# A planned four-layer graph kernel: seven more turns of 128x512 tiles by VectorE and DMA in place of TensorE, with new planning constants

## The chip, the cores and the metric

The kernel runs on one core of one Trainium2 chip. The metric is the device time of one execution in microseconds, as the median of several runs. Everything is float32.

## The reference

The input x has 64 graphs of 256 nodes with 128 features, and all graphs share one symmetric 256x256 adjacency matrix. Four layers follow one another, each as x = layernorm(x + layer(x)):

```python
# layer 0: attention whose logits come from pairs of nodes, softmax over axis 1
h = x @ Wo; att = softmax(where(adj > 0, leaky(u1[idx1] + u2[idx2]), NEG), axis=1)
out0 = att @ h + x @ Wself
# layer 1: attention with source and target terms, then elu
att = softmax(where(adj + I == 0, NEG, leaky(es[:, None] + ed[None, :])))
out1 = elu(att @ (x @ W))
# layer 2: five steps of a gated recurrent cell, with m = adj @ h in both halves of av
z = sigmoid(av @ w3.T + h @ u3.T); r = sigmoid(av @ w4.T + h @ u3.T)
h = (1 - z) * h + z * tanh(av @ w5.T + (r * h) @ u5.T)
# layer 3: x W0 + sums of adj^k x Wk, k = 1, 2, 3, once for each of two adjacencies (here the same)
```

## The kernel before

**Units and lanes.** Two graphs make a unit: 512 rows of 128 features, 32 units (NU), which take their buffers from ten lanes (unit u uses lane u % 10). Ten units are open at a time; when one ends, the next of its lane begins, and its x is loaded when its predecessor's tasks have been spawned.

**The planner.** The kernel first writes down every instruction of a unit as a task with an engine, an estimated duration and its dependencies (`Plan.add`, L94). `Plan.run` (L156) then plays the five queues (TensorE, VectorE, ScalarE, GpSimd and SP, which issues the DMAs) forward in estimated time, and on each engine that is free takes the ready task with the smallest key. The order it writes out is the program's order on every engine; the hardware then runs each engine in that order and waits where data isn't there. The key is made by `first` (L1184): the unit's number times PERIOD (for the last ten units a value that differs by only TAIL = 0.3 of a PERIOD from unit to unit), plus the task's due time, minus HASTE for the engines that HASTE names, if the task lies between the first and the last use of a PSUM bank (`within`). The due time is the estimated length of the chain before the task in its unit, times PACE (PACE_GATED in layer 2). Setup tasks that are wanted late have a rank in place of the key. LATENCY is the assumed time from an instruction's end to where its result can be used, 4000 ns for a DMA; in the first 35 us (START) the shorter table EARLY is used. TURN is added to a VectorE task of the kind [...], if the one before it was of that kind too.

**Two layouts.** A state is used with rows on the partitions (as the stationary operand of a product with the adjacency) and with features on the partitions (for the products with weights). So states are turned again and again, in one of two ways:

- By TensorE: four transposes of 128x128 into a PSUM bank and one ScalarE copy out of it (`feature_major`, L590, whose transposes are L593 and whose copy is L595; in layer 2, L1031 and L1034).
- By VectorE and DMA ("far"): a VectorE transpose of 32x32 blocks (L606, L1006 or L1019), a store to a DRAM buffer hb (L609, L1009 or L1024), and loads that bring the blocks to their places (four of 64 KB at L612 or L1012; one at L1027 behind four stores).

`far(u, step)` (L585) says which way a unit takes at a step. Step -1 is the turn into layer 2, steps 0 to 4 are those of layer 2, step 5 is the turn into layer 3. All units are far at all steps, but units 0 and 1 only from step 2 on (FIRST_FAR), and unit 31 only at steps below 1, that is -1 and 0 (LAST_FAR).

**The input.** `load_x` (L360) brings a unit's x into the lane's buffer m. Units below XDIRECT = 10 load it in one DMA with rows on the partitions (L364); layer 0 turns it by TensorE (L713). From unit 10 on, four DMAs (L368) bring it in with its 32-wide blocks placed so that one VectorE transpose (L714) finishes the turn. The loads of units 0 to 9 are in the setup, before other work on SP. Unit 0's goes out on ScalarE's queue. In layer 0, L727 multiplies x with the weights, L798 and L803 make the output; on units from 3 on, small vectors are spread over the partitions through DRAM rows (L620, L624, L743).

**Filler.** `warm` (L401) issues 256-wide matmuls of the identity (L405), four at the start and six that carry a rank behind all else.

**Layer 2.** In each of five steps m = adj @ h is made in one of two ways. Where `far(u, step - 1)` holds, `left_fast` (L899) takes seven 128-wide products (L904) with three block sums on GpSimd (L893, L895, L896) and merges (L936 to L939); else `left` (L877) takes four 256-wide ones (L881) and a ScalarE copy (L959). Five 512-wide products with the gates' weights follow (L963), with three tanh on ScalarE and four VectorE updates.

**Layer 3.** Its products with the weights and with the squared adjacency are made in one of two ways. Units below NU - PLAIN = 28 use `layer3_blocks` (L1064): 21 products of 128 columns (L1088), with seven GpSimd operations (L1080, L1121 to L1123), seven copies (L1099) and VectorE sums (L1102, L1135). Units 28 to 31 use `layer3_end` (L1148): eight 256-wide products with the weights (L1157), two copies (L1161) and four 256-wide products (L1164). The last two units end with `layernorm_last` (L683), in halves.

Of the kernel before, what the change touches and what calls it, by code (L numbers as in the profile page):

```python
# [28 lines left out]
DIRECT_D = 3  # L29
WARM = 6  # L30
FIRST_FAR = {0: 2, 1: 2}
LAST_FAR = {0: 1}
PERIOD = 41000.0
TAIL = 0.3
LATE = 5
PACE = 4.0
PACE_GATED = 1.56
HOLD = 80
DIRECT_ROWS = 3
XDIRECT = 10  # L40
START = 35e3
HASTE = {"pe": 45000.0, "act": 45000.0}
IN_PSUM = (0, 1, 0, 1)
MARGIN = {}
TURN = 12000.0
PLAIN = 4
R2 = 1
R3 = 1.5

# [25 lines left out]
class Plan:  # L75
# [2 lines left out]

    LATENCY = {"pe": 400, "dve": 350, "act": 350, "pool": 900, "sp": 4000}

    EARLY = {"pe": 250, "dve": 180, "act": 200, "pool": 250, "sp": 2500}
    OWN = {"pe": 0, "dve": 70, "act": 70, "pool": 100}
# [71 lines left out]
    def run(self, spawn, units, key):  # L156
# [23 lines left out]
        def start(lane):  # L180
            mine = [u for u in queue if u % LANES == lane]
            if mine:
# [5 lines left out]
                for t in self.tasks[seen:]:  # L188
                    t.due = max([d.due + (PACE_GATED if t.layer == 2 else PACE) * (d.ns + (
                        d.wait + self.LATENCY["sp" if d.dma else d.eng] if d.dma or d.eng != t.eng else self.OWN[t.eng]))  # L190
                        for d in t.deps if d.unit == t.unit], default=0.0)
# [6 lines left out]
        while any(ready.values()) or running:  # L198
# [11 lines left out]
            for e, tasks in ready.items():  # L210
# [4 lines left out]
                if not fit:  # L215
                    continue
                t = min(fit, key=lambda t: key(t) + (TURN if twice and t.port and e == "dve" else 0))
                if t.at > now:
# [10 lines left out]
                if t.port:  # L229
                    held[e] = t.off - 65 if e == "dve" else begin + 50 if t.ns > 900 else t.off - 125  # L230
                t.end = t.off + (self.EARLY if now < START else self.LATENCY)["sp" if t.dma else e] + t.wait
                done_at[t] = t.end
# [18 lines left out]
def kernel(  # L251
# [108 lines left out]
    def load_x(u, by="sp"):  # L360
        z = lanes[u % LANES]["m"]
        if u < XDIRECT:
            queue = {"sp": nc.sync, ACT: nc.scalar}[by]
# [209 lines left out]
    def gd(ap):  # L573
        return ap.rearrange("p (g d) -> p g d", g=G)
# [10 lines left out]
    def far(u, step):  # L585


        return step >= FIRST_FAR.get(u, -1) and step < LAST_FAR.get(NU - 1 - u, STEPS + 1)

    def feature_major(src, view, t):  # L590
        ps = bank()
        for g in range(G):
            add(PE, 110, lambda g=g: nc.tensor.transpose(ps.ap[:, g * P : (g + 1) * P], view(g), ident.ap),  # L593
                (src, ident), (ps,))
        add(ACT, 475, lambda: nc.scalar.copy(t.ap, ps.ap), (ps,), (t,))  # L595
# [113 lines left out]
    def layer0(u, L):  # L709
        xT, z = L["xT0"], L["m"]  # L710
        if u < XDIRECT:
            feature_major(z, lambda g: gd(z.ap)[:, g], xT)
# [333 lines left out]
    def layer3(u, L):  # L1046
# [10 lines left out]

        if u >= NU - PLAIN:
            layer3_end(u, L, xT, aT, s, tail)
# [88 lines left out]
    def layer3_end(u, L, xT, aT, s, tail):  # L1148
        ps = [bank() for _ in range(NC)]

        def view(c):
            return ps[c].ap.rearrange("p (k b d) -> p k b d", k=2, b=UB)

        for k, src in enumerate((xT, aT)):
            for c in range(NC):
                for b in range(UB):
                    add(PE, mm_ns(N), lambda k=k, src=src, c=c, b=b: nc.tensor.matmul(  # L1157
                        view(c)[:, :, b, :], bn(src.ap)[:, b, c * P : (c + 1) * P], w3.ap[:, k],
                        start=(k == 0 and b == 0), stop=(k == 1), skip_group_check=True), (src, w3), (ps[c],), tail)
        for c in range(NC):  # L1160
            add(ACT, 300, lambda c=c: nc.scalar.copy(s.ap[:, c * N : (c + 1) * N], ps[c].ap[:, N : 2 * N]), (ps[c],), (s,), group=ps)  # L1161
        for c in range(NC):
            for mc in range(NC):
                add(PE, mm_ns(N), lambda c=c, mc=mc: nc.tensor.matmul(  # L1164
                    ps[c].ap[:, 0:N], a2T.ap[:, mc, c * P : (c + 1) * P], s.ap[:, mc * N : (mc + 1) * N],
                    start=False, stop=(mc == NC - 1), skip_group_check=True), (a2T, s), (ps[c],))
        pairs = [(ps[c], lambda c=c: view(c)[:, 0]) for c in range(NC)]
        if u >= NU - 2:
            layernorm_last(u, pairs)
            return  # L1170
        layernorm(u, L, pairs, swap=True)
        add("sp", 450, lambda: nc.sync.dma_start(out_u[u], X[u].ap), (X[u],), ())
# [10 lines left out]
    def first(t):  # L1183
        if t.rank is not None:  # L1184
            return t.rank * PERIOD
        if t.unit < 0:
            return t.due - 1e6
        soon = HASTE.get(t.eng, 0) if t.within else 0
        return (t.unit if t.unit < NU - LANES else NU - 1 - LATE - (NU - 1 - t.unit) * TAIL) * PERIOD + t.due - soon
# [34 lines left out]
```

The softmax here doesn't subtract the row's maximum and nothing guards it: scores larger than these inputs give would overflow.

## Time and profile before

| what | value |
|---|---|
| median of 3 runs | 1382.91 us (1382.16 to 1383.07) |
| the profiled execution | 1382.03 us |
| its span, first to last instruction | 1380.2 us, granted TensorE clock 1.00 |
| TensorE busy | 1371.9 us (99%), 7221 instructions |
| VectorE, ScalarE, GpSimd busy | 1167.7 (85%), 972.2 (70%), 691.3 us (50%) |
| DMA | 147.21 MB, 107 GB/s; q1, SP's queue, 46.8% of 16 engines |
| layer 2's weight products (L963), 1600 instructions | 593 ns a record |
| transposes of x in layer 0 (L593 on m), 40 instructions | 273 ns a record |
| VectorE transposes of x (L714), 22 | 0.70 us each |

An f32 matmul appears as two instructions, a transpose as one. Records of TensorE overlap, since matmuls are pipelined, and their ends are modelled: what an instruction costs TensorE is the distance to the start of the next one. A timeline row merges neighbours of the same kind: start, time to the end of the last of them, engine, line, operation, names, shape, count, and in brackets the idle time of the engine before it. In the table of stretches, the columns after the stretch's length are the busy us (and instructions) of TensorE, its weight loads, VectorE, ScalarE and GpSimd, then the granted clock, the DMA share and GB/s. A buffer's number is left out of its name, so units are told apart by time and line only.

### The profile page before, as it was taken

How to read it: one execution, taken by the hardware profiler on the slowest of the kernel's cores; microseconds unless marked ns; L12 is line 12 of the kernel's file. 1: busy time of each engine (PE TensorE's matmuls, PEld its weight loads, DVE VectorE, ACT ScalarE, POOL GpSimd, SP SyncE). 2: the span in 40 equal slices, each digit the busy share in tenths (PEclk: the TensorE clock that was granted, in tenths of full speed). 3: DMA queues.
4: the chain of work that ended last, by engine and by line, in shares of the span. 5: the costliest groups of instructions: out<-in, count | busy, mean ns of one | idle time of the engine just before them, and what ended most of it. 6: DMA issues, size and time to landing. Idle time of an engine off the chain costs nothing.

```text
span 1380.2 us, 24466 instructions
## 1 busy us (share of the span) xinstructions
PE 1371.9 (99%) x7221; PEld 970.5 (70%) x7221; DVE 1167.7 (85%) x2709; ACT 972.2 (70%) x2414; POOL 691.3 (50%) x1240
## 2 busy tenths in 40 slices
PE   9999999999999999999999999999999999999998
PEld 9767676676676776767767667776666676667777
DVE  7968988988888888899888998888888787889854
ACT  6897676756776777778777767788766656566555
POOL 5214473544554664556545564565545433446814
PEclk9999999999999999999999999999999999999999
DMA  4223454454455455454555455545555443645412
GB/s 128 56 55 89 105 117 114 98 126 106 107 131 108 92 117 137 109 118 105 109 126 119 112 111 110 109 107 134 119 114 117 90 103 84 131 111 117 109 47 69
DMA packets 530084, 147.21 MB, mean 107 GB/s; under 512 B 456480, under 2 KB 495136, under 8 KB 529952
## 3 DMA queue, kind: packets, MB, share of 16 engines
q1 hardware_dynamic: 529152, 145.13, 46.8%
q8 instruction: 58, 0.95, 0.3%
q14 instruction: 74, 0.61, 0.2%
q10 hardware_dynamic: 800, 0.52, 0.1%
HBM read 81.10 MB, written 64.46 MB: 105 GB/s over the span
## 4 chain that ended last, share of the span: by engine, by line
PE 98%; DVE 1%; ACT 0%; issue 0%; POOL 0%; POOLq 0%; DVEq 0%; ACTq 0%
PE ps L963 50%; PE ps L904 20%; PE ps L1088 10%; PE ps L840 4%; PE ps L803 4%; PE ps L727 2%; PE ps L852 2%; PE ps L798 2%; PE ps L881 1%; PE ps L1157 1%; PE ps L1164 0%; PE ps L405 0%; PE ps L593 0%; PE ps L1031 0%; PE ps L636 0%; PE ps L752 0%
## 5 line engine op out<-in xcount | busy, mean ns | idle before, releaser
L963 PE MATMUL ps<-m,gT 128*128 128x512 f32 x960 | 473.3, 593 | 0.0
L963 PEld LDWEIGHTS ps<-m,gT 128*128 128x128 f32 x960 | 168.0, 191 | 131.8 <-issue 114.4
L975 ACT ACTIVATE e<-ps,bias 128x512 f32<-128x512 f32 x160 | 109.8, 687 | 94.7 <-PE ps L963 85.8
L649 POOL TENSOR_SCALAR ve<-st 128x4 f32<-128x4 f32 x110 | 26.8, 244 | 278.4 <-DVE st L647 269.6
L963 PE MATMUL ps<-e,u5T 128*128 128x512 f32 x320 | 163.5, 592 | 0.0
L904 PEld LDWEIGHTS ps<-adjTp,ht 128*128 128x128 f32 x726 | 118.6, 191 | 61.2 <-issue 48.6
L652 POOL TENSOR_TENSOR rstd<-ve,nhalf 128x4 f32<-128x4 f32 x126 | 137.5, 1091 | 47.5 <-DVE ve L649 41.4
L993 ACT ACTIVATE p<-ps,bias 128x512 f32<-128x512 f32 x160 | 109.9, 687 | 66.6 <-PE ps L963 64.2
L904 PE MATMUL ps<-adjTp,e 128*128 128x128 f32 x968 | 149.0, 276 | 0.2 <-ACT m L919 0.2
L984 ACT ACTIVATE ps<-ps,bias 128x512 f32<-128x512 f32 x160 | 105.6, 661 | 55.1 <-PE ps L963 54.3
L893 POOL TENSOR_TENSOR e<-ht 128x256 f32<-128x256 f32 x121 | 96.9, 801 | 88.1 <-DMA ht<-hb 73.1
L904 PEld LDWEIGHTS ps<-adjTp,e 128*128 128x128 f32 x968 | 129.6, 192 | 11.9 <-issue 7.9
L996 DVE SCALAR_TENSOR_TENSOR ps<-ps,p 128x512 f32<-128x512 f32 x160 | 110.2, 689 | 32.0 <-ACT p L993 31.4
L904 PE MATMUL ps<-adjTp,ht 128*128 128x128 f32 x726 | 136.7, 275 | 0.0
L963 PEld LDWEIGHTS ps<-e,u5T 128*128 128x128 f32 x320 | 58.7, 190 | 63.1 <-issue 55.5
L963 PE MATMUL ps<-xT,gT 128*128 128x512 f32 x192 | 98.2, 593 | 0.0
L671 ACT ACTIVATE x<-ht,ve,rstd 128x128 f32<-128x128 f32 x208 | 91.1, 490 | 5.1 <-POOL ve L660 5.0
L936 DVE TENSOR_TENSOR m<-ps,m 128x256 f32<-128x256 f32 x182 | 74.8, 413 | 14.1 <-PE ps L904 12.8
L829 ACT ACTIVATE e<-m,esd 128x256 f32<-128x256 f32 x116 | 84.6, 769 | 0.0
L978 DVE SCALAR_TENSOR_TENSOR e<-e,xT 128x512 f32<-128x512 f32 x96 | 72.2, 752 | 12.9 <-ACT e L975 12.4
L893 POOL TENSOR_TENSOR e<-x 128x256 f32<-128x256 f32 x61 | 48.6, 797 | 65.5 <-ACT x L671 57.7
L919 ACT COPY m<-ps 128x128 f32<-128x128 f32 x182 | 48.0, 268 | 44.0 <-PE ps L904 35.0
(219 smaller groups left out, 3356.1 us busy)
## 6 DMA issues: line engine op xcount, KB each, us to landing
hb<-p SPq DMA_DIRECT2D x182, 256.0 KB, 2.3
ht<-hb SPq DMA_DIRECT2D x484, 64.0 KB, 2.6
xT<-hb SPq DMA_DIRECT2D x244, 64.0 KB, 2.6
m<-row SPq DMA_DIRECT2D x58, 256.0 KB, 3.7
hb<-p SPq DMA_DIRECT2D x124, 64.0 KB, 1.8
ht<-hb SPq DMA_DIRECT2D x31, 256.0 KB, 2.8
out_dram<-x SPq DMA_DIRECT2D x30, 256.0 KB, 2.4
m<-in_x_dram SPq DMA_DIRECT2D x88, 64.0 KB, 2.4
```

Of the source, the lines that this page charges most:

```text
L652: add(POOL, 1010, lambda: nc.gpsimd.tensor_tensor(rstd.ap, ve.ap, nhalf.ap, op=ALU.pow), (ve, nhalf), (rstd,))
L671: add(ACT, 400, lambda j=j, b=b, ch=ch, view=view, at=at, shift=shift, col=col: nc.scalar.activation(X[u].ap[:, b, ch, :], view()[:, j, :] ...
L829: add(ACT, 660 if u >= DIRECT_ROWS else 360, lambda g=g, b=b: nc.scalar.activation(e.ap[:, g, :].rearrange("p (c n) -> p c n", c=NC), ev() ...
L893: add(by, wide, lambda: eng.tensor_sub(four[:, 0:2], blk(slice(2, 3)).to_broadcast([P, 2, D]), blk(slice(0, 4, 3))), (src,), (s,), group=s ...
L904: add(PE, mm_ns(P) + 4, lambda: nc.tensor.matmul(ps.ap[:, at * P : (at + 1) * P], lhs(), mat.ap[:, k, c * P : (c + 1) * P], start=start, s ...
L936: add(DVE, 335, lambda: nc.vector.tensor_tensor(mv[:, 1:3], pv(y)[:, 0:2], mv[:, 3:4].to_broadcast([P, 2, P]), op=ALU.add), (y, m), (m,))
L963: add(PE, mm_ns(T), lambda: nc.tensor.matmul(ps.ap, w(), rhs.ap, start=start, stop=stop, skip_group_check=True), (c, rhs), (ps,), after)
L975: add(ACT, 590, lambda ps_g=ps_g, up=up, tr=tr: nc.scalar.activation(tr.ap, ps_g.ap, AF.Tanh, bias=bias2.ap[:, 1:2], scale=0.5 / up), (ps_ ...
L984: add(ACT, 590, lambda ps_g=ps_g, up=up, tz=tz: nc.scalar.activation(tz.ap, ps_g.ap, AF.Tanh, bias=bias2.ap[:, 0:1], scale=0.5 / up), (ps_ ...
L993: add(ACT, 590, lambda ps_v=ps_v, up=up, tv=tv: nc.scalar.activation(tv.ap, ps_v.ap, AF.Tanh, bias=bias2.ap[:, 2:3], scale=1 / up), (ps_v, ...
L996: add(DVE, 600, lambda tz=tz, tv=tv, vv=vv: nc.vector.scalar_tensor_tensor(vv.ap, tz.ap, 1.0, tv.ap, op0=ALU.add, op1=ALU.mult), (tv, tz), ...
L1088: nc.tensor.matmul(part(ps, at)[:, 0], l(), r(), start=start, stop=True, skip_group_check=True)
```

## The change

Seven constants are changed:

```diff
-LAST_FAR = {0: 1}
+LAST_FAR = {0: 3}
...
-PACE = 4.0
+PACE = 3.0
...
-XDIRECT = 10
+XDIRECT = 5
 START = 35e3
-HASTE = {"pe": 45000.0, "act": 45000.0}
+HASTE = {"pe": 70000.0, "act": 70000.0, "dve": 70000.0}
 IN_PSUM = (0, 1, 0, 1)
 MARGIN = {}
-TURN = 12000.0
-PLAIN = 4
+TURN = 0
+PLAIN = 3
...
-    LATENCY = {"pe": 400, "dve": 350, "act": 350, "pool": 900, "sp": 4000}
+    LATENCY = {"pe": 400, "dve": 350, "act": 350, "pool": 900, "sp": 3500}
```

Three of them change instructions. With XDIRECT = 5 the x of units 5 to 9 comes in by four DMAs and is turned by VectorE (L368 and L714) in place of one DMA, four transposes and a copy. With LAST_FAR = 3 unit 31 is far at steps 1 and 2 too: the states after these steps are turned by VectorE and DMA, and steps 2 and 3 use `left_fast`. With PLAIN = 3 unit 28 uses `layer3_blocks`. The other four (PACE, HASTE, TURN and the DMA entry of LATENCY) enter only the planner's estimates and keys, so the order of the instructions on every engine is another one throughout.

## The prediction

> **What bounds the kernel now.** I read the page first: the busy line and the chain that ended last.
>
> ```profile
> PE 1371.9 (99%) x7221; PEld 970.5 (70%) x7221; DVE 1167.7 (85%) x2709; ACT 972.2 (70%) x2414; POOL 691.3 (50%) x1240
> ...
> PE 98%; DVE 1%; ACT 0%; issue 0%; POOL 0%; POOLq 0%; DVEq 0%; ACTq 0%
> ```
>
> TensorE is busy for all but 8.3 us of the 1380.2 us span, and the chain stays on it for 98%. Of the 8.3 us, 1.34 lie before its first matmul and about 5.6 behind its last (the last normalization and its store); only some 1.4 lie inside the run. So the forecast is one of TensorE work removed, plus what the new order does at the two ends, where work is scarce. Busy time alone doesn't say that TensorE is full, so I took the spacing of its instructions from its timeline at the end of the run:
>
> ```profile
> 1359.28 0.60 PE L593 MATMUL ps<-ident,x 128*128 128x128 f32 x4
> 1359.72 1.89 PE L881 MATMUL ps<-adjT,x 128*128 128x256 f32 x8
> 1361.45 1.89 PE L1157 MATMUL ps<-w,xT 128*128 128x256 f32 x8
> 1363.17 2.32 PE L1157 MATMUL ps<-w,m 128*128 128x256 f32 x10
> ```
>
> The first column is the start. Four transposes take 1359.72 - 1359.28 = 0.44 us, 0.109 each; eight 256-wide instructions take 1.73, 0.216 each (a plain f32 matmul is two instructions, so 0.432 a matmul). In the same view six 128-wide ones start at 1356.64 and the next at 1357.31: 0.112 each. Those are my prices for TensorE, and not the 273 to 382 ns that single records show, which overlap.
>
> Next the busy time by stretch (us in 10: TensorE, its weight loads, VectorE, ScalarE, GpSimd):
>
> ```profile
> 20.00:30.00 10.00, 10.00 (x92) 10.00 (x91) 8.65 (x31) 7.83 (x24) 6.08 (x12) 1.00 0.04 4
> 30.00:40.00 10.00, 9.93 (x81) 9.49 (x80) 8.51 (x25) 8.64 (x25) 3.96 (x5) 1.00 0.36 74
> 40.00:50.00 10.00, 10.00 (x52) 8.00 (x51) 10.00 (x35) 8.50 (x24) 1.86 (x5) 1.00 0.06 10
> 80.00:90.00 10.00, 10.00 (x44) 6.08 (x43) 6.86 (x13) 10.00 (x25) 0.00 (x1) 1.00 0.13 42
> 1340.00:1350.00 10.00, 10.00 (x47) 7.17 (x46) 5.13 (x13) 4.66 (x10) 2.72 (x6) 1.00 0.09 28
> ```
>
> At 40 to 50 us VectorE is full. At 1340 us it has half its time free. What TensorE does at 36 to 48 us:
>
> ```profile
> 36.35 3.79 PE L727 MATMUL ps<-wx,xT 128*128 128x133 f32 x32
> 39.97 1.03 PE L405 MATMUL ps<-ident 128*128 128x256 f32 x4
> 40.87 1.97 PE L840 MATMUL ps<-p,x 128*128 128x256 f32 x8
> 42.67 0.59 PE L405 MATMUL ps<-ident 128*128 128x256 f32 x2
> 43.10 0.60 PE L636 MATMUL ps<-ident,esd 128*128 128x128 f32 x4
> 43.54 0.60 PE L405 MATMUL ps<-ident 128*128 128x256 f32 x2
> ...
> 47.46 0.59 PE L405 MATMUL ps<-ident 128*128 128x256 f32 x2
> ```
>
> L405 is filler: matmuls of the identity with the lowest rank of all, taken only when the plan has nothing else. Twelve instructions run between 39.97 and 47.9, 12 x 0.216 = 2.6 us. So there TensorE looks full and is short of work. From 48 us on there is no filler, and the work is real.
>
> **What the Trainium skill says.** "TensorE: Matmul & The Clock Gate", section "Part 4: PE-mode transpose", gives about 275 ns for a 128x128 transpose in a kernel. The records here agree (273 ns), but the spacing, 109 ns, is what a removed one gives back. "VectorE: DVE Perf Modes", "The three transpose paths": VectorE turns 32x32 blocks only, so a full turn needs a second step, here DMA through HBM; its row costs 0.70 us per 128x512 state. "DMA: Bandwidth & Descriptors", "Anatomy of one DMA": about 2 us fixed, mostly completion. The trace agrees: 2.3 us to landing for hb<-p and 2.6 for ht<-hb.
>
> **The change, part by part.**
>
> XDIRECT 10 to 5. Units 5 to 9 lose 5 x 4 transposes: 20 x 0.109 = 2.18 us of TensorE, and 5 copies of 0.586 us (L595), 2.9 us of ScalarE. They gain five VectorE transposes (L714, 0.701): 3.5 us. On SP's queue five loads become twenty; 20 x 0.487 (median of L368) = 9.7 us replace the 3.45 us that five take from 11.21, so the queue ends near 21 us instead of 14.7. What stands behind them is the first row store, at 27.49: 6 us of cover. Without it, row stores and what waits for them would be up to 6 us late. The loads land 2.4 us later, near 23.5; the DMA share at 20 to 30 us is 0.04, so smaller pieces have room. The x of these units is wanted by the L727 matmuls at 36.35. Were it late, the transpose would wait on VectorE, and the first units' softmax and normalization rows, queued behind it, with it. Cost: nothing. On TensorE the 20 transposes stand at 28.5 to 30.4 (16 of them), ahead of the starved stretch, so their removal can just widen it. Bounds for this part: a gain of 2.18 if real work moves up (ScalarE, which is 10.0 of 10 at 80 to 90 us, has lost 2.9), a loss of 3.5 if every added VectorE transpose stands on the chain to the first units. I take a gain of half, **1.09**.
>
> LAST_FAR 1 to 3. In the last unit the states after steps 1 and 2 go by VectorE and DMA: 8 transposes less, 8 x 0.109 = **0.87 us**, and 2 copies of 0.59 on ScalarE. VectorE gains 2 x 0.70, SP 2 x 5 issues (0.33 + 4 x 0.63 = 2.9 us each) among its other transfers. It also makes steps 2 and 3 use the seven-product scheme: 14 instructions of 0.112 (1.57) for 8 of 0.216 (1.73), twice: **0.32 us**. GpSimd gains three sums a step (0.80 + 0.52 + 0.54). TensorE had no visible wait from 1320 to 1370 us, so I count both as whole.
>
> PLAIN 4 to 3. Unit 28 takes the block form of layer 3: 42 x 0.112 = 4.70 us for 24 x 0.216 = 5.18: **0.48 us**. GpSimd gains 5 x 0.73 + 2 x 0.46 = 4.6 us, VectorE about 2.4, ScalarE 2.4 - 0.74; at half load they hide it while other units are there. If not, that chain of some ten dependent steps lengthens unit 28 by a few us, before units that end later.
>
> Order (PACE, HASTE, TURN, the assumed DMA latency). It adds no instruction. It moves every wait. The inside waits are 1.4 us as shown, so the gain is bounded by that and perhaps 2 us hidden in the modelled ends. A loss isn't bounded by the page; 0.3 us in each of 22 stretches of 60 us would be 6.6. The assumed DMA latency falls from 4.0 to 3.5 us after the issue; with 2.6 us from issue to landing that is still long enough. HASTE brings forward what ends a bank's use; TURN = 0 lets VectorE take two port-sharing operations in a row, which can hold up GpSimd; 50% busy, GpSimd is no bound. I take half of the visible waits, a gain of **0.7 us**.
>
> Sum: 1.09 + 0.87 + 0.32 + 0.48 + 0.7 = 3.46 us. The profiled execution took 1382.03 (span 1380.2 and 1.83 around it) and becomes 1378.6. It lay 0.9 below the median of 1382.91, so for the median I say **1379.4**.
>
> **The rivals.**
>
> *The last unit starves TensorE (slower).* Turned by TensorE, its state after step 1 needs 1.77 us to the next product with the adjacency:
>
> ```profile
> 1310.81 0.60 PE L1031 MATMUL ps<-ident,xT 128*128 128x128 f32 x4
> ...
> 1312.58 1.89 PE L881 MATMUL ps<-adjT,ht 128*128 128x256 f32 x8
> ```
>
> By DMA, from SP's timeline:
>
> ```profile
> 1296.76 0.45 SPq L1009 DMA_DIRECT2D hb<-p  x1
> ...
> 1299.43 3.10 SPq L1012 DMA_DIRECT2D ht<-hb  x4
> ```
>
> With the VectorE transpose at 1295.07 and 2.6 us of landing behind 1302.5, this is 10 us; where the queue was free (1282.80 to about 1291) 8.2. So 6.4 to 8.2 us more, twice, and about 2 us a step for GpSimd's sums and the merging: 17 to 20 us. Queued behind the store that waits are the other units' transfers on SP. The slack of this unit: its steps take 12.9 to 14.0 us (1310.81, 1323.67, 1337.71, 1351.62), and the rows of one in a chain (1.73 adjacency, 0.59 copy, 0.86 gate, 0.66 tanh, 0.75, 0.86, 0.69 tanh, 0.69, 0.68, 0.44 transposes, 0.59 copy: 8.5) with waits of about 0.2 between them come near 10, so 3.2 x 3, and some 2.4 before layer 3: 12 us. If the order doesn't bring unit 31 forward by the rest, 5 to 8 us are idle at the end: 1379.4 + 6.5 = 1386, up to 1391 if the slack is not used. It decides when unit 31 reaches its step-1 state later than some 5 us before today's 1310.8. For it: five units are left then, and a longer chain gives later due times. Against: unit 31 has 3 x 6.5 us of steps (0.44 + 1.73 + 10 x 0.429) and 7.4 of layer 3 on TensorE from there to its last matmul at 1374.6, so 37 of those 64 us are other units' work and can fill. 0.18.
>
> *The start is bound by chains (no change).* The filler says so. Then XDIRECT gives nothing or up to half the added VectorE time: 1382.91 - 1.67 + 0 to 1.8 = 1381.2 to 1383.0, say **1381.6**. 0.18.
>
> *The order is looser in the body.* 6.6 us as above on 2.8 saved: **1386.7**. Nothing in the page of before speaks for or against, except that 1.4 us of waits leaves more room above than below. 0.10.
>
> That the settings don't take hold can be left out: each is a plain test on a unit's number.
>
> **How the numbers follow.** The forecast has 0.54, with its own range 1376 to 1380.5. Its tight end: 1382.91 - 3.85 - 1.4 - 1.7 = 1376. About 0.2%, 2.8 us, is what a measurement tells from no change, so faster means below 1380.1, slower above 1385.7. Faster: nearly all of the forecast and a little of the start's rival, 0.55. Within: the rest of these, 0.18. Slower: the tail and the loose order, 0.27. The range of 8 in 10 runs from 1376 to 1388; above it lies the worse half of the slower cases.
>
> **What would show it.** L593 on m should fall from 40 records to 20 and L714 rise from 22 to 27; L1031 from 32 to 24; L881 from 80 to 64; L1157 from 64 to 48. TensorE's instruction count falls by 28 + 16 + 24 and rises by 28 + 42. Right: those counts, no new idle time of TensorE at 10 to 60 us and in the last 60, and a busy sum some 3.8 us smaller. Wrong at the start: more filler, or gaps ahead of L840 and L636 behind VectorE rows. Wrong at the end: TensorE idle with ht<-hb as the releaser after 1300 us. Wrong in the order: waits spread over all stretches.

## The result, and the profile after

| | before | after |
|---|---|---|
| median of 20 runs each, same chip | 1382.24 us | 1384.62 us (1383.58 to 1385.71) |
| ratio | | 1.0017 (95%: 1.0010 to 1.0024) |
| profiled span | 1380.2 us | 1381.9 us |

The change costs 2.4 us where the forecast was a gain of 3.5. The bound named in the prediction, 0.2% or 2.8 us, calls this no change; the interval says that it is a small loss.

The page after, the busy line and the shares of the chain that ended last:

```profile
PE 1369.6 (99%) x7223; PEld 967.5 (70%) x7223; DVE 1171.3 (85%) x2731; ACT 968.6 (70%) x2414; POOL 695.0 (50%) x1253
...
PE 96%; DVE 2%; ACT 1%; issue 0%; POOL 0%; POOLq 0%; DVEq 0%; ACTq 0%
```

TensorE's busy sum fell by 2.3 us and the span rose by 1.7: the chain now spends 3% of the span (VectorE 2, ScalarE 1) off TensorE, where it was 1%. The edits did what they say: in the groups by line, L593 on m fell from 40 to 20, L714 rose from 22 to 27, L1031 fell from 32 to 24, L881 from 80 to 64, L1157 from 64 to 48. The stretches shown of before, again (columns as there):

```profile
20.00:30.00 10.00, 8.24 (x73) 7.98 (x72) 9.81 (x34) 6.43 (x18) 5.96 (x11) 1.00 0.40 61
30.00:40.00 10.00, 9.65 (x71) 8.99 (x71) 9.80 (x26) 8.27 (x24) 0.94 (x3) 1.00 0.23 57
40.00:50.00 10.00, 9.38 (x56) 7.50 (x55) 10.00 (x34) 7.26 (x18) 3.88 (x6) 1.00 0.00 0
80.00:90.00 10.00, 10.00 (x44) 6.00 (x43) 9.20 (x25) 10.00 (x25) 0.00 (x0) 1.00 0.28 50
1340.00:1350.00 10.00, 9.78 (x60) 7.71 (x60) 5.50 (x13) 6.69 (x18) 7.03 (x14) 1.00 0.29 74
```

TensorE, the first column after the length, was 10.0, 9.9 and 10.0 of 10 from 20 to 50 us and is now 8.2, 9.7 and 9.4. VectorE, the third, is at 9.8 or more in all three, where it was 8.7, 8.5 and 10.0. TensorE's waits by releaser (total us, times, longest):

```profile
PE ps L727 <- DVE xT L714: 1.8, 1, 1.8
PE ps L405 <- POOL ident masks.py:199: 1.3, 1, 1.3
PE ps L904 <- ACT m L919: 0.7, 3, 0.3
PE ps L904 <- ACT e L916: 0.7, 3, 0.2
PE ps L963 <- ACT xT L595: 0.6, 1, 0.6
PE ps L840 <- DVE p L833: 0.4, 1, 0.4
```

The longest new wait is for L714, the very transpose that the change adds. Where it stands on TensorE:

```profile
26.45 0.60 PE L636 MATMUL ps<-ident,esd 128*128 128x128 f32 x4
28.81 2.08 PE L727 MATMUL ps<-wx,xT 128*128 128x133 f32 x16 [1.76 <-DVE xT L714]
30.73 0.60 PE L636 MATMUL ps<-ident,esd 128*128 128x128 f32 x4
31.68 1.99 PE L840 MATMUL ps<-p,x 128*128 128x256 f32 x8 [0.35 <-DVE p L833]
...
42.49 2.32 PE L405 MATMUL ps<-ident 128*128 128x256 f32 x10
44.65 0.60 PE L636 MATMUL ps<-ident,esd 128*128 128x128 f32 x4
45.08 0.60 PE L405 MATMUL ps<-ident 128*128 128x256 f32 x2
...
48.47 1.12 PE L963 MATMUL ps<-xT,gT 128*128 128x512 f32 x2 [0.62 <-ACT xT L595]
```

There are 12 instructions of filler (L405) after 40 us, as before. Twenty transposes are gone from TensorE, and still the first product of layer 2 (L963) starts at 48.47 us, where it started at 47.90. On VectorE, at the same time:

```profile
27.87 0.24 DVE L734 SCALAR_TENSOR_TENSOR cu<-cu 128x4 f32<-128x4 f32 x2
28.05 1.31 DVE L714 STREAM_TRANSPOSE xT<-m 128x512 f32<-128x512 f32 x2
29.28 1.08 DVE L675 TENSOR_SCALAR x<-ps,rstd 128x128 f32<-128x128 f32 x4
...
32.62 1.89 DVE L714 STREAM_TRANSPOSE xT<-m 128x512 f32<-128x512 f32 x3
```

No bracket stands behind them: VectorE was not waiting for x, it was busy with the first units' softmax and normalization rows and came to these transposes late. Nor was it the loads, as SP's queue shows:

```profile
11.46 12.85 SPq L368 DMA_DIRECT2D m<-in_x_dram  x20
28.06 0.35 SPq L620 DMA_DIRECT2D row<-cu  x1
```

They were issued until 24.3 us, later than the 21 of the prediction (0.64 us each in a row, not 0.487), and landed 3.0 us after their issue (the median of the twenty), before VectorE came to them; the next issue stood at 28.06 anyway.

**Where the time went.** Short gaps on TensorE don't show as waits, so I measured spacing. For each line of TensorE I took the distance from one start to the next, and as the usual one the value that a fifth of them lie below; what a distance has beyond it is a gap. The usual distances add up to the work.

| us | work | gaps 0 to 60 us | gaps 60 to 1320 | gaps from 1320 | last matmul's start to the end |
|---|---|---|---|---|---|
| before | 1359.2 | 3.6 | 10.9 | 0.5 | 5.96 |
| after | 1355.0 | 6.8 | 12.2 | 1.4 | 6.51 |
| difference | -4.2 | +3.2 | +1.3 | +0.9 | +0.55 |

The sum is +1.8, for +1.7 of span. So the TensorE work that the prediction counted (2.18 + 0.87 + 0.32 + 0.48 = 3.85) did go, and came back as gaps, most of it at the start.

### The profile page after: what moved, and what is told of

Its sections match the earlier page's. It is cut to its first block, busy times and chain, and to the rows that moved or that the text cites. A ratio compares the mean times of both kernels' runs of the same rounds, so it can differ in the third digit from the quotient of the medians.

```text
span 1381.9 us, 24601 instructions
## 1 busy us (share of the span) xinstructions
PE 1369.6 (99%) x7223; PEld 967.5 (70%) x7223; DVE 1171.3 (85%) x2731; ACT 968.6 (70%) x2414; POOL 695.0 (50%) x1253
## 4 chain that ended last, share of the span: by engine, by line
PE 96%; DVE 2%; ACT 1%; issue 0%; POOL 0%; POOLq 0%; DVEq 0%; ACTq 0%
PE ps L963 50%; PE ps L904 21%; PE ps L1088 10%; PE ps L840 4%; PE ps L803 4%; PE ps L798 2%; PE ps L852 2%; PE ps L727 2%; PE ps L881 1%; PE ps L1157 1%; PE ps L405 0%; PE ps L1164 0%; DVE e L766 0%; PE ps L1031 0%; ACT ht L782 0%
## 5 line engine op out<-in xcount | busy, mean ns | idle before, releaser
L963 PE MATMUL ps<-m,gT 128*128 128x512 f32 x960 | 477.9, 593 | 0.0
L963 PEld LDWEIGHTS ps<-m,gT 128*128 128x128 f32 x960 | 166.5, 191 | 128.2 <-issue 109.9
L963 PE MATMUL ps<-e,u5T 128*128 128x512 f32 x320 | 163.4, 592 | 0.0
L904 PE MATMUL ps<-adjTp,e 128*128 128x128 f32 x984 | 153.8, 276 | 0.7 <-ACT m L919 0.7
L652 POOL TENSOR_TENSOR rstd<-ve,nhalf 128x4 f32<-128x4 f32 x126 | 134.9, 1071 | 27.0 <-DVE ve L649 20.5
L904 PEld LDWEIGHTS ps<-adjTp,e 128*128 128x128 f32 x984 | 133.4, 192 | 19.5 <-issue 14.8
L904 PE MATMUL ps<-adjTp,ht 128*128 128x128 f32 x738 | 139.9, 275 | 0.0
L963 PEld LDWEIGHTS ps<-e,u5T 128*128 128x128 f32 x320 | 59.0, 190 | 65.5 <-issue 52.8
L963 PE MATMUL ps<-xT,gT 128*128 128x512 f32 x192 | 98.3, 594 | 0.6 <-ACT xT L595 0.6
L936 DVE TENSOR_TENSOR m<-ps,m 128x256 f32<-128x256 f32 x184 | 75.9, 413 | 24.8 <-PE ps L904 24.3
L671 ACT ACTIVATE x<-ht,ve,rstd 128x128 f32<-128x128 f32 x212 | 93.3, 491 | 3.1 <-POOL ve L660 3.1
L904 PE MATMUL ps<-adjT,e 128*128 128x128 f32 x488 | 77.6, 276 | 0.7 <-ACT e L916 0.7
```

The source lines that it names most:

```text
L652: add(POOL, 1010, lambda: nc.gpsimd.tensor_tensor(rstd.ap, ve.ap, nhalf.ap, op=ALU.pow), (ve, nhalf), (rstd,))
L671: add(ACT, 400, lambda j=j, b=b, ch=ch, view=view, at=at, shift=shift, col=col: nc.scalar.activation(X[u].ap[:, b, ch, :], view()[:, j, :] ...
L904: add(PE, mm_ns(P) + 4, lambda: nc.tensor.matmul(ps.ap[:, at * P : (at + 1) * P], lhs(), mat.ap[:, k, c * P : (c + 1) * P], start=start, s ...
L936: add(DVE, 335, lambda: nc.vector.tensor_tensor(mv[:, 1:3], pv(y)[:, 0:2], mv[:, 3:4].to_broadcast([P, 2, P]), op=ALU.add), (y, m), (m,))
L963: add(PE, mm_ns(T), lambda: nc.tensor.matmul(ps.ap, w(), rhs.ap, start=start, stop=stop, skip_group_check=True), (c, rhs), (ps,), after)
```

## The experiments

My theory after this reading: the start is bound by chains through VectorE (theory A where an expectation uses the letter), so XDIRECT costs time there, and the rest is the new order. Its rivals: the start is full on TensorE and the loss is the order's alone (theory B); or the end is what lost. Two kinds of experiment tell them apart. In the first the order of before is kept, instruction for instruction, and one thing is exchanged in place. In the second the planner makes its order anew.

### With the order of before kept: the start

**f0_nopet.** A task `turn_early` takes the place of TensorE's turn of x in units 5 to 9:

```diff
-            feature_major(z, lambda g: gd(z.ap)[:, g], xT)
+            feature_major(z, lambda g: gd(z.ap)[:, g], xT) if u < 5 else turn_early(z, xT, bank())
+ # turn_early: four empty TensorE tasks, then nc.scalar.copy(t.ap, z.ap)
```

> The kernel before, its order on every engine kept, with the 20 transposes of units 5 to 9 left out on TensorE (the five ScalarE copies stay and copy x unturned, so what these five units compute is not the reference's). Theory A, the start is bound by chains through VectorE and TensorE only fills there: these 20 transposes are worth nothing, 0 to 0.4 us faster, and TensorE shows about 2 us of idle time between 28 and 48 us. Theory B, TensorE is the bound from the first microseconds on: 2.2 us faster, no new idle time.

Measured: 1381.68 us against 1382.26 for before, ratio 0.9998 (0.9989 to 1.0006). TensorE's timeline in before:

```profile
28.53 1.91 PE L593 MATMUL ps<-ident,m 128*128 128x128 f32 x16
30.51 1.99 PE L840 MATMUL ps<-p,x 128*128 128x256 f32 x8
...
47.90 1.02 PE L963 MATMUL ps<-xT,gT 128*128 128x512 f32 x2
```

And without the twenty transposes:

```profile
28.30 0.39 PE L727 MATMUL ps<-wx,xT 128*128 128x133 f32 x2
30.49 1.99 PE L840 MATMUL ps<-p,x 128*128 128x256 f32 x8 [1.81 <-DVE p L833]
...
47.83 1.02 PE L963 MATMUL ps<-xT,gT 128*128 128x512 f32 x2
```

L840 starts at 30.49 in place of 30.51. Of the time that sixteen transposes filled, 1.81 us has become a wait for the row L833 on VectorE, layer 2 starts only 0.07 us earlier, and the gaps up to 60 us grow by 2.0. The interval alone would still allow a gain of 1.5 us; it is the trace that puts the removal at next to nothing.

**f2_dve.** The other half alone: TensorE keeps its transposes, and VectorE gets five more, into a buffer that nothing reads.

```diff
-        add(ACT, 475, lambda: nc.scalar.copy(t.ap, ps.ap), (ps,), (t,))
+        add(ACT, 475, lambda: [nc.scalar.copy(t.ap, ps.ap)] + ([nc.vector.transpose(extra.ap, src.ap)] if extra else []), (ps,), (t,))
```

> The kernel before, order kept, all its work kept, and five more VectorE transposes of 128x512 (3.5 us in all) put beside the ScalarE copies of units 5 to 9, into a buffer that nothing reads. Theory A: VectorE is on the chain, so 1.5 to 3.5 us slower, with TensorE idle between 28 and 48 us. Theory B: under 0.5 us slower.

Measured: 1383.15 us against 1382.26, ratio 1.0006 (1.0000 to 1.0013), +0.9 us, less than the 1.5 to 3.5 expected under theory A; the first L963 at 48.54. The five in its groups by line, 10 to 40 us (count, then busy us and mean ns):

```profile
L595 DVE STREAM_TRANSPOSE p<-m 128x512 f32<-128x512 f32 x5 | 3.5, 696 | 0.0
```

3.5 us more on VectorE delay layer 2 by 0.64 us and the end by 0.9. TensorE's work is unchanged here, so this comes from the added VectorE rows.

**f1_kept.** Both halves: the XDIRECT part of the change whole, with the four loads of L368 in place of L364's one.

```diff
+ # turn_early as in f0_nopet, with nc.vector.transpose(t.ap, z.ap) in place of the copy
```

> The kernel before, order kept, with the first part of the change alone: units 5 to 9 come in by four DMAs each and are turned by VectorE in the place of the ScalarE copies; their TensorE transposes and these copies are gone. Theory A: 1 to 3.5 us slower than before, with no new plan at all. Theory B: 2.2 us faster, since the transposes are off TensorE and the loss of the changed kernel came from its new order.

Measured: 1383.05 us against 1382.26, ratio 1.0006 (0.9998 to 1.0014), +0.8 us, just under the range of theory A. L840 waits 1.76 us for L833 as in f0_nopet, the first L963 is at 49.37, and the gaps up to 60 us are 7.45 us: 3.88 more than before, for 2.2 of work less (2.8 by the table's usual distances). Single intervals of these three touch 1, but that of f1_kept leaves no room for the gain of 1.09 us that was forecast (a ratio of 0.9992). Together with the traces they put XDIRECT, in the order of before, at a loss near 0.8 us.

### With the order of before kept: the end

**f5_tail.** Eight transposes of the last unit's states left out, as LAST_FAR does, with nothing in their place but a ScalarE copy.

```diff
+ # L1031: no transpose, L1034: copy h itself, for u == NU - 1 and step in (1, 2)
```

> The kernel before, order kept, with the 8 transposes of the last unit's states after steps 1 and 2 left out on TensorE (the two ScalarE copies copy the states unturned, so the last unit's output is not the reference's). If TensorE is the bound there, as the prediction said: 0.87 us faster. If the last unit's own chain is the bound: also faster, by up to 0.87, and not told apart; if neither, because other waits take over: 0 to 0.3.

Measured: 1381.49 us against 1382.14, ratio 0.9996 (0.9987 to 1.0004), -0.65 us; the profiled span is 1379.3, 0.9 less. The eight transposes were priced at 0.87. The interval touches 1, but the value, the span and TensorE's gaps from 1320 us (0.5 as before) agree with an end that TensorE binds. A last unit bound by its own chain would look the same here, as the expectation says.

### One part at a time, order made anew

| | edit to before | us (before 1382.02; p4_order 1382.14) | ratio (95%) | gaps 0 to 60 | 60 to 1320 | from 1320 | to the end |
|---|---|---|---|---|---|---|---|
| p1_x | XDIRECT 5 | 1396.45 | 1.0105 (1.0090 to 1.0120) | 6.8 | 17.3 | 7.8 | 5.89 |
| p2_last | LAST_FAR 3 | 1397.73 | 1.0114 (1.0097 to 1.0131) | 3.1 | 11.2 | 17.3 | 6.06 |
| p3_plain | PLAIN 3 | 1384.33 | 1.0016 (1.0009 to 1.0023) | 3.7 | 10.8 | 1.0 | 8.25 |
| p4_order | the four planning constants | 1391.33 | 1.0066 (1.0053 to 1.0078) | 5.6 | 16.6 | 1.0 | 7.37 |

> The kernel before with XDIRECT 5 alone, planned anew. With the order kept this part cost 0.8 us. If a new plan can make up for it, as the prediction took: 1.1 us faster than before. If a new plan is a draw: 1 to 10 us slower, with some 3 us more gaps in the first 60 us and the rest spread over the body.

> The kernel before with LAST_FAR 3 alone, planned anew with the old constants. If it is the last unit's longer chain that starved TensorE in the run with the old constants (13.5 us of gaps in the last 60): 10 to 20 us slower than before, the gaps after 1320 us. If that came from another part: 3 to 9 us slower with the gaps in the body, or 1.2 us faster.

> The kernel before with PLAIN 3 alone, planned anew. It alters only unit 28, so the order of the first two thirds should be that of before: 0.5 us faster if TensorE bounds the end, up to 1 us slower if the block form's chain ends late. A loss over 2 us would show a new draw at the end.

> The kernel before with the four new planning constants alone. If they are worse in themselves: 2 to 4 us slower than before. If they are better, as the prediction took: 0.7 us faster. If an order is a draw with a spread of some us: anywhere from 1 us faster to 5 slower, and with gaps at other places than in the changed kernel.

No part alone gains. **p1_x** and **p4_order** are other orders throughout, and can't be read as the price of a part; both lost more than any expectation named (14.4 us where at most 10 stood, 9.2 where at most 5). **p2_last** keeps the body of before (11.2) and loses it all at the end. TensorE's waits from 1320 us on:

```profile
PE ps L593 <- ACT x L671: 4.0, 1, 4.0
PE ps L1031 <- DVE p L998: 2.3, 1, 2.3
PE ps L904 <- ACT e L916: 2.2, 1, 2.2
```

These are the steps of a unit's own chain (normalization before the turn into layer 3, a state's update before its turn, a merge before the seven products): the last unit runs alone, and TensorE starves. Unit 31 was not brought forward (which unit a row belongs to is read from the order that the planner writes): VectorE turns its state after step 1 at 1309.38 us, where TensorE did it at 1310.81 in before, and the state after step 3 comes 25.7 us later than the 1337.71 of before:

```profile
1363.37 0.65 PE L1031 MATMUL ps<-ident,xT 128*128 128x128 f32 x4
```

**p3_plain** keeps the order of before until its last hundred or so TensorE rows. Its work is 0.6 us less, its last matmul ends at 1374.57 (before 1374.65), and 7.9 us lie behind that (before 5.6). The timeline of its end, ScalarE and SP:

```profile
1373.00 5.32 SPq L702 DMA_DIRECT2D out_dram<-x  x3
...
1377.09 0.48 ACT L671 ACTIVATE x<-ht,ve,rstd 128x128 f32<-128x128 f32 x1
1377.48 0.44 ACT L696 ACTIVATE x<-ps,ve,rstd 128x128 f32<-128x128 f32 x1
1377.82 1.25 ACT L671 ACTIVATE x<-ht,ve,rstd 128x128 f32<-128x128 f32 x3
1379.10 0.37 SPq L1146 DMA_DIRECT2D out_dram<-x  x1
```

The last store is L1146, a store of the block form, and in the order that the planner writes it is unit 28's: this unit, now in that form, ends after units 30 and 31 (L702), its normalization (L671) sharing ScalarE with theirs. This is the case that the prediction named as the loss of cover and set at nothing. The expectation had read a loss over 2 us as a new draw at the end; the gaps from 1320 us are only 0.5 more, and the tail carries the 2.3 us.

### From the changed kernel backwards

**m_order**: the changed kernel with the four planning constants of before. **m_x**: the changed kernel with XDIRECT 10.

> The changed kernel with the four planning constants of before (PACE 4, HASTE for TensorE and ScalarE only, TURN 12000, 4000 ns for a DMA). If the new constants are what made the order worse: 2 to 4 us faster than the changed kernel (1380.5 to 1382.5), with body gaps of about 11 us. If the loss came from the start and from planning noise, the same within 2 us either way (1382.6 to 1386.6).

> The changed kernel with XDIRECT back at 10, planned anew. Theory A: the gaps of TensorE in the first 60 us go back from 6.8 to about 3.6 us while 2.2 us of transposes come back, so 1 us faster than the changed kernel or equal to it (1383.2 to 1384.6), and the gaps elsewhere stay as large, since they come with the order. Theory B: 2.2 us slower than the changed kernel (1386.8).

m_order: 1403.69 us, 1.0157 (1.0143 to 1.0171), far above both expectations. Its gaps from 1320 us are 16.2. One of its stretches (TensorE first, the granted clock third from the end):

```profile
1360.00:1370.00 10.00, 5.25 (x10) 2.32 (x10) 3.55 (x5) 5.54 (x13) 3.41 (x8) 0.83 0.19 52
```

Half of TensorE's time is idle, the granted clock falls to 0.83 on the mean, and no other engine is above 5.6 of 10: a chain alone. With the old constants, then, the rival of the starving last unit happens; in the changed kernel it does not. There VectorE turns unit 31's states after steps 1 and 2 at 1275.68 and 1306.64 us; TensorE turned them at 1310.81 and 1323.67 in before. The unit was brought forward by 35 us where the longer chain begins (the prediction had asked for some 5), and its state after step 3 is turned where it was before, at 1337.71:

```profile
1337.61 0.60 PE L1031 MATMUL ps<-ident,xT 128*128 128x128 f32 x4
```

TensorE's only visible waits from 1300 us on are two of 0.2 us. The new constants don't ensure this: n2_after, below, has them too, and 8.2 us of gaps from 1320 us, 2.8 of them one wait for the last unit's normalization.

m_x: 1388.25 us, 1.0046 (1.0033 to 1.0058), 3.6 above the changed kernel. Neither number that I had named (theory B's 1386.8 is the nearer); its gaps are 6.2 at the start, 15.7 in the body and 1.3 at the end. So with the new constants the start has 2.6 us more of gaps even with XDIRECT 10 (p4_order: 2.0), and with XDIRECT 5 alone 3.2 (p1_x). Either is enough for most of the +3.2 of the change, and they don't add.

### Is an order a draw?

The same instructions with a constant moved by 0.1% to 0.7%, on before and on the changed kernel.

```diff
-PERIOD = 41000.0
+PERIOD = 41050.0    n1_before, n2_after
+PERIOD = 41100.0    n5_before, n6_after
-PACE = 4.0          (3.0 in the changed kernel)
+PACE = 3.98         n3_before
+PACE = 2.98         n4_after
```

> The kernel before with PERIOD 41050 in place of 41000. If every order is a draw and that of before a good one: 3 to 10 us slower than before, with gaps at other places. If only the changed kernel's constants make orders that fragile: within 1 us of before.

> The changed kernel with PERIOD 41050 in place of 41000, a change of 0.12% that has no meaning of its own but makes a new order from the middle of the program's first third on. If the order of the body is a draw: differs from the changed kernel by 1 us or more in either direction. If the body's waits follow from the constants: within 0.5 us of it (1384.1 to 1385.1).

> The kernel before with PACE 3.98 in place of 4.0: 0.5% on one term of the key, no instruction added. If the orders of before and after are two lucky draws out of a wide spread, this lands 5 to 15 us above 1382, as the change of PERIOD by 0.12% did (+10.9). If PERIOD was a special case and the order follows the constants smoothly, it stays within 1 us of 1382.

> The changed kernel with PACE 2.98 in place of 3.0. Wide spread: 5 to 15 us above 1384.6. Smooth: within 1 us of it.

> The kernel before with PERIOD 41100 in place of 41000 (0.24%). Wide spread: 5 to 15 us above 1382, and not the 1392.9 of PERIOD 41050. Smooth: between 1382 and 1393 would need a slope, some 1400 here. With the next one and the others: if the changed instructions save their 3.9 us on the mean of the draws, the mean of the draws of after lies some 4 us below that of before; if the start eats it, they are level.

> The changed kernel with PERIOD 41100. Wide spread: 5 to 15 us above 1384.6 and unlike the 1393.5 of PERIOD 41050. Smooth: 1402.

| | us | ratio to before (95%) | gaps 0 to 60 | 60 to 1320 | from 1320 |
|---|---|---|---|---|---|
| before | 1382.24 | | 3.6 | 10.9 | 0.5 |
| n1_before | 1392.88 | 1.0079 (1.0064 to 1.0094) | 3.5 | 20.4 | 1.5 |
| n3_before | 1393.72 | 1.0086 (1.0057 to 1.0116) | 3.2 | 22.4 | 1.3 |
| n5_before | 1390.97 | 1.0069 (1.0046 to 1.0092) | 3.5 | 19.0 | 1.6 |
| after | 1384.62 | 1.0017 (1.0010 to 1.0024) | 6.8 | 12.2 | 1.4 |
| n2_after | 1393.55 | 1.0083 (1.0069 to 1.0097) | 7.6 | 16.1 | 8.2 |
| n4_after | 1382.82 | 1.0008 (0.9998 to 1.0018) | 7.2 | 11.5 | 0.7 |
| n6_after | 1387.78 | 1.0039 (1.0020 to 1.0059) | 7.7 | 15.7 | 1.3 |

Five of the six tweaks, which alter nothing but the order, cost 3 to 12 us; one gains 1.8. n4_after and n6_after fall outside both of their expectations. In n3_before TensorE (first after the length) loses 8 us in one third of the body:

```profile
360.00:720.00 360.00, 359.32 (x1930) 254.01 (x1929) 314.74 (x714) 265.34 (x673) 201.03 (x362) 1.00 0.51 114
720.00:1080.00 360.00, 351.96 (x1848) 245.39 (x1847) 303.11 (x693) 260.29 (x657) 188.63 (x345) 1.00 0.50 109
```

The granted clock is the same in both and the DMA share nearly so, and the edit alters nothing but the order. (In n1_before and n5_before the clock is halved once in the body, for 3.4 us from 419 and 418 us on, which costs at most 1.7.) Two things can be told from the table. **The start** is settled: the gaps there are 3.2 to 3.6 in all four orders of before and 6.8 to 7.7 in all four of the changed kernel. **The body** is a draw: 10.9 to 22.4 and 11.5 to 16.1. The orders of before scatter over 11.5 us and those of the changed kernel over 10.7, so the +2.4 between the two measured kernels lies well inside what an order is worth. n4_after has the same edits and is level with before. The mean of the four orders is 1390.0 us for before and 1387.2 for the changed kernel; with this scatter, 2.8 us between two means of four don't decide between the 4 us and the level means that n5_before's expectation named.

Over all the orders made anew, the gaps up to 60 us go by XDIRECT and the constants like this:

| gaps 0 to 60 us | XDIRECT 10 | XDIRECT 5 |
|---|---|---|
| constants of before | 3.1 to 3.8 (before, n1, n3, n5, p2_last, p3_plain) | 6.8 (p1_x), 6.1 (m_order) |
| new constants | 5.6 (p4_order), 6.2 (m_x) | 6.8 to 7.7 (after, n2, n4, n6) |

XDIRECT 5 has 2.2 us less work there. With the constants of before it brings 2.4 to 3.8 us of gaps, a loss; with the new ones only 0.7 to 2.1, so there it is no loss. The new constants bring some 2 to 3 us of their own where XDIRECT is 10. What is settled for the changed kernel is the start as a whole, 3.2 us of gaps for 2.2 of work; how much of the loss belongs to which depends on the one that is put in first.

## Why the prediction was wrong

- **XDIRECT, a gain of 1.09: this step failed, in its sign.** The prediction saw the filler and VectorE full, said that the removal "can just widen" the starved stretch, and then took half of the gain as a compromise between bounds. In the order of before, f0_nopet puts the removal at next to nothing, f2_dve the added VectorE rows at a cost of 0.9, f1_kept both at +0.8. In the changed kernel the start loses about 1 us (3.2 of gaps for 2.2 of work), where a gain of 1.09 was forecast; the new constants have a share in that. The rival of the chain-bound start had the mechanism and, at 0 to 1.8 lost, the size; it deserved to be the forecast of this step. VectorE was at 8.65 and 8.51 of 10 from 20 to 40 us: that looked like room, but the rows that others wait for stood in the same queue as the new ones.
- **SP's queue, cost nothing: right**, though its end (24.3 us) was put at 21. That left 3.7 us of cover before the next issue in place of 6, and it was enough.
- **LAST_FAR, 0.87 and 0.32.** The price of the transposes was right (f5_tail: 0.65 by the runs, 0.9 by the spans). It rests on the spacing of 0.109 us; the 275 ns that the prediction quotes from the Trainium skill ("TensorE: Matmul & The Clock Gate", section "Part 4: PE-mode transpose") belong to bf16 there, and these transposes are float32. The seven-product term wasn't separated. The rival was real with the old constants (p2_last: +15.7, twice to three times the 5 to 8 us of idle time that I worked out), and the order of the changed kernel removed it, by starting the unit's longer chain 35 us earlier. There the gain of the end was given back by small gaps (+0.9) and a longer tail (+0.55): the prediction didn't ask what a denser end costs. Four stores (L702) are issued in a row from 1377.56 us on, where before had two at 1371.13 and two at 1376.86, since the last two units now end together.
- **PLAIN, 0.48.** The work fell by 0.6 in p3_plain, so the term was right on TensorE; the cover named for unit 28's chain wasn't there (+2.3 behind the last matmul). In the changed kernel no L1146 store comes later than the L702 ones: this loss wasn't paid there.
- **Order, a gain of 0.7: this step failed too.** It was bounded by visible waits (1.4 us). But before has 10.9 us of gaps in the body that no wait shows, and its order is the best of its four by 8.7 us. A new order had about 10 us to lose and little to gain; what the measured one did (+1.3 in the body) was lucky. And at the start the new constants alone bring 2.0 to 2.6 us of gaps (p4_order, m_x). The rival of the looser order had the right mechanism: of the twelve other orders made anew, ten have over 6.6 us more gaps than before on all stretches together, though only four in the body alone.

In sum: 3.9 to 4.2 us of TensorE work went, 3.2 came back at the start, 1.4 at the end, 1.3 in the body. Open is what decides where an order falls in the body. With the old constants, the new orders have 17.3 to 22.4 us of gaps there (n1, n3, n5, p1_x, m_order: 18.5), with the new ones 11.5 to 16.6 (n2, n4, n6, p4_order, m_x). That suggests that the new constants are the better ones apart from before's own lucky draw, but five draws of each don't show it for other settings. No version here beats before: f0_nopet and f5_tail leave work out, and n4_after is within its interval.

## What to carry to other kernels

Filler in a busy engine was the sign that the stretch belongs to someone else. Ask first which engine is late there: a removal from the filled one gave next to nothing here, and 3.5 us added to the late one cost 0.9, though it showed 15% idle. Where a planner writes the order, move a constant by 0.1% a few times before an edit is judged, since the scatter of the order can be larger than the edit; and exchange instructions in place, with the order kept, to price an edit by itself. When work is taken out near the end, follow what lies behind the last matmul as well: a unit that gets a longer chain can become the last to store.

## What the runs showed of the hardware

- **A thinly used TensorE can cost more than its idle time.** In m_order TensorE waited 2.90 us for ScalarE; the next four L963 instructions took 2.73 us and the two after them 1.65, where four take 1.72 and two 0.86 at full clock:

```profile
1362.53 2.94 PE L963 MATMUL ps<-m,gT 128*128 128x512 f32 x4 [2.90 <-ACT e L975]
1365.26 1.81 PE L963 MATMUL ps<-e,u5T 128*128 128x512 f32 x2
1366.91 0.39 PE L904 MATMUL ps<-adjT,x 128*128 128x128 f32 x2
```

  The Trainium skill, "TensorE: Matmul & The Clock Gate", section "Part 1: The HAM clock gate", says that the clock is halved after an idle window of about 3.4 us. The traces agree on the length and not on the idleness. The granted clock that they record is 0.50 in m_order from 1363.4 to 1366.8 and from 1370.3 to 1373.7 us, so twice for 3.4. Up to the last matmul, every length at full or half clock is a whole multiple of 3.41 us (in p2_last 1348.3, 3.4, 20.5, 6.8 and 10.2). Counted in such stretches over all runs, the clock was halved only after one in which TensorE's records fill at most 1.74 us (0.89 and 1.04 in m_order, 1.54 and 0.66 in p2_last), and never after one with 1.8 or more (between 1.6 and 1.8 both occurred). So a stretch that is busy for less than about half was enough; it need not be idle. At half speed m_order lost at most 3.4 us, and p2_last, halved for 10.2 us, at most 5.1: part of their 16 and 17 us of gaps, and a cost that the starving rival had left out.
- **Twenty loads in a row** on SP took 0.64 us each to issue; the median of L368 over the run is 0.487.
